# A selective-scan block: sums over the state issued in threes, one PSUM bank for states, nine of 24 products on GpSimd

## The chip, the cores and the metric

The kernel runs on one core of a Trainium2 chip. The metric is the device time of one execution in microseconds, the median of several runs. A profile is one further execution, taken by the hardware profiler.

## The reference, cut to what matters

The model has several blocks one after another on an input of 4 images, 96 channels, 64 x 64 pixels. The change lies in the first one, a selective scan over the 4096 pixels in four directions (K=4, rows, columns and both backwards), for 192 channels (DI) with 16 states each (N):

```python
def step(hst, inp):
    ut, dt_, bt, ct = inp
    dA = jnp.exp(dt_[..., None] * A[None])
    hst = hst * dA + (dt_ * ut)[..., None] * bt[:, :, None, :]
    y = jnp.einsum('bkdn,bkn->bkd', hst, ct)
    return (hst, y)
h0 = jnp.zeros((b, K, DI, N), jnp.float32)
_, ys = jax.lax.scan(step, h0, (u_t, d_t, B_t, C_t))
```

`delta` and u give the decay exp(delta A) and the input delta u B of each state; y is the sum over the 16 states of the state times C. The four directions are added, normalised over the channels and projected back to 96 channels. A block of three convolutions (1x1 to 576 channels, 3x3 by channel, 1x1 back) follows; then come a spectral block, an attention block and two feed-forward blocks, which the change doesn't touch.

## The kernel before, in words

For each of the four images, `scan_block` makes u by a convolution on TensorE (lines 230 to 254), then `scan_chunks` does the scan, `scan_output` the normalisation and projection, and `conv_block` the convolutions. After the four images the rest of the model runs image by image (line 698 on). 

`scan_chunks` works through 32 steps an image: 4 directions, each with 8 chunks of 512 pixels. A tile of 128 partitions holds 32 channels with 4 states each, so a step has 24 tiles: j runs over the four groups of states, i over the six groups of channels, t = 6 j + i. For each t (lines 347 to 367):

- ScalarE writes exp(delta A) into a PSUM bank `da` (line 353; two banks, names `ps_da`);
- GpSimd multiplies delta u with B into `db` (line 355; three buffers);
- VectorE scans h = h da + db along the 512 pixels (line 357). For the t in `POOL_C` (seven of 24) the state h goes to SBUF (`hs`, two buffers), for the others to a PSUM bank (`ps_h`, two banks);
- ScalarE copies the last column of h into `after`, the start of the next chunk (line 362; not in the last chunk of a direction);
- h is multiplied with C into `hc` (line 364; three buffers), on GpSimd for the t in `POOL_C`[...], on VectorE for the others;
- TensorE multiplies `hc` with a constant of 128 x 32 that adds the four states of each channel, and adds up over j in PSUM (line 367): the channels of i go to the quarter 32 (i mod 4) of the 128 columns, in bank `y01` for i under 4 and in `y2` for 4 and 5.

At a step's end VectorE adds `y01` and `y2` to the sums `ya` and `yb` over the directions (lines 373 and 374). Beside a step, `prepare` makes delta and delta u of the next one: matmuls into banks `mm` (lines 286, 287 and 297), ScalarE's copy and softplus (lines 289 and 300 to 302), two VectorE instructions for each half of the channels (lines 304 and 306), and writes to DRAM; from there they and B and C are loaded again, spread over the partitions (lines 315 and 323), from SP's queue.

Nobody writes out the order of the instructions. The program gives each engine's operations with their data, and a scheduler orders each engine's queue ahead of time: of the instructions that it holds for ready it takes the one that comes earliest in the program. It takes a free buffer for each tile, or makes the first writer wait for the release of an old one. In the run each engine follows its queue in this fixed order.

[...] Before, the function `bank` takes two for each name unless it is told otherwise: `mm`, `da` and `h` two each, `y01` and `y2` one each. `h` also serves `scan_output` (the variance, lines 390 and 391) and `conv_block` (the 3x3 convolution of two of the five tiles on TensorE, line 434), and `mm` the sums of the last convolution (line 448).

Of the kernel before, what the change touches and what calls it, by code (L numbers as in the profile page):

```python
# [17 lines left out]
F32 = mybir.dt.float32  # L18
# [13 lines left out]
CH = 512  # L32
# [2 lines left out]
NTOK = L // 128  # L35
NI, NJ = DI // 32, NS // 4
NE1 = NE + 1
POOL_C = (2, 5, 9, 12, 16, 19, 23)
ROWS1 = [128, 128, 128, 128, 64]
PE_CONV = (0, 1)  # L40

# [33 lines left out]
def hybrid_kernel(ctx: ExitStack, tc: tile.TileContext, a: dict):  # L75
# [40 lines left out]
    with tc.tile_pool(name="ca", bufs=1) as ca, tc.tile_pool(name="xa", bufs=1) as xa, tc.tile_pool(  # L116
        name="psa", bufs=2, space=PSUM
    ) as psa, tc.tile_pool(name="dr", bufs=3, space=bass.MemoryType.DRAM) as dr:
        def bank(tag, bufs=None):
            return psa.tile([128, CH], F32, name=f"ps_{tag}", tag=tag, bufs=bufs)  # L120

        cst = ca.tile([128, NCA], F32, name="cst_a")
        nc.sync.dma_start(cst, a["cst_a"])
# [154 lines left out]
        def scan_chunks(ua, ub, ya, yb, wk):  # L278

            steps = [(k, n, NCH - 1 - n if k >= 2 else n) for k in range(K) for n in range(NCH)]  # L280

            def prepare(at):

                k, _, c = steps[at]
                p = bank("mm")
                mm(p[:NE], lhsT=sel_a[:, k, :], rhs=view(ua, k, c), start=True, stop=False)
                mm(p[:NE], lhsT=sel_b[:, k, :], rhs=view(ub, k, c), start=False, stop=True)
                xd = xds[at % 2]
                nc.scalar.copy(xd[:NE], p[:NE])  # L289
                bc = dr.tile([2 * NS, CH], F32, name="dram_bc")  # L290
                nc.sync.dma_start(bc, xd[: 2 * NS])
                delta = dr.tile([DI, CH], F32, name="dram_delta")
                du = dr.tile([DI, CH], F32, name="dram_du")
                for u, lo, hi in ((ua, 0, 128), (ub, 128, DI)):
                    m = hi - lo
                    p = bank("mm")
                    mm(p[:m], lhsT=dtw[:, k, lo:hi], rhs=xd, start=True, stop=True)  # L297

                    z = wk.tile([m, CH], F32, name=f"z{lo}", bufs=1)
                    act(z, p[:m], AF.Abs)  # L300
                    act(z, z, AF.Exp, scale=-1.0)
                    act(z, z, AF.Ln, bias=1.0)
                    d = wk.tile([m, CH], F32, name=f"delta{lo}", bufs=1)
                    nc.vector.scalar_tensor_tensor(d, p[:m], 0.0, z, ALU.max, ALU.add)
                    g = wk.tile([m, CH], F32, name=f"du{lo}", bufs=1)
                    nc.vector.tensor_mul(split(g), split(d), view(u[:m], k, c))
                    nc.sync.dma_start(delta[lo:hi], d)
                    nc.sync.dma_start(du[lo:hi], g)
                return {"bc": bc, "delta": delta, "du": du, "B": {}, "C": {}, "d": {}, "g": {}}

            def load_states(s, j):

                for name, at in (("B", 4 * j), ("C", NS + 4 * j)):
                    t = wk.tile([128, CH], F32, name=f"rep_{name}", bufs=5)
                    nc.sync.dma_start(t, s["bc"][at : at + 4].unsqueeze(0).to_broadcast([32, 4, CH]))
                    s[name][j] = t

            def load_channels(s, i):

                for name, of in (("d", "delta"), ("g", "du")):  # L320
                    t = wk.tile([128, CH], F32, name=f"rep_{name}", bufs=9)
                    src = s[of][32 * i : 32 * i + 32].unsqueeze(1).to_broadcast([32, 4, CH])
                    nc.sync.dma_start(t, src)
                    s[name][i] = t

            def first_loads(s):
                load_states(s, 0)
                for i in range(NI // 2):
                    load_channels(s, i)

            cur = prepare(0)
            first_loads(cur)
            for j in range(1, NJ):
                load_states(cur, j)
            for i in range(NI // 2, NI):
                load_channels(cur, i)
            before = None
            for at, (k, n, c) in enumerate(steps):
                nxt = None
                if at + 1 < len(steps):  # L340
                    nxt = prepare(at + 1)
                    first_loads(nxt)
                order = slice(None, None, -1) if k >= 2 else slice(None)
                end = 0 if k >= 2 else CH - 1
                after = wk.tile([128, NI * NJ], F32, name="state") if n < NCH - 1 else None
                y01, y2 = bank("y01", 1), bank("y2", 1)
                for j in range(NJ):
                    for i in range(NI):
                        t = j * NI + i
                        pool_c = t in POOL_C  # L350
                        av = (k * NI + i) * NJ + j
                        da = bank("da")
                        act(da, cur["d"][i], AF.Exp, scale=aneg[:, av : av + 1])  # L353
                        db = wk.tile([128, CH], F32, name="db", bufs=3)
                        nc.gpsimd.tensor_mul(db, cur["g"][i], cur["B"][j])  # L355
                        h = wk.tile([128, CH], F32, name="hs") if pool_c else bank("h")
                        nc.vector.tensor_tensor_scan(  # L357
                            h[:, order], da[:, order], db[:, order],
                            0.0 if n == 0 else before[:, t : t + 1], ALU.mult, ALU.add,
                        )  # L360
                        if after is not None:
                            nc.scalar.copy(after[:, t : t + 1], h[:, end : end + 1])  # L362
                        hc = wk.tile([128, CH], F32, name="hc", bufs=3)
                        (nc.gpsimd if pool_c else nc.vector).tensor_mul(hc, h, cur["C"][j])  # L364
                        y = y01 if i < 4 else y2
                        q = 32 * (i % 4)
                        mm(y[q : q + 32], lhsT=cst[:, CA["stack"]], rhs=hc, start=j == 0, stop=j == NJ - 1)  # L367
                        if nxt is not None and j == NJ - 1 and i < NI // 2:
                            load_channels(nxt, NI // 2 + i)
                    if nxt is not None and j < NJ - 1:  # L370
                        load_states(nxt, j + 1)
                before = after
                nc.vector.tensor_add(view(ya, k, c), view(ya, k, c), split(y01))
                nc.vector.tensor_add(view(yb[:64], k, c), view(yb[:64], k, c), split(y2[0:64]))
                cur = nxt

        def scan_output(xt, ya, yb, wk):

            for c in range(NCH):
# [6 lines left out]
                qb = wk.tile([128, CH], F32, name="qb", tag="rep_g", bufs=9)  # L386
                act(qa, pa, AF.Square)
                act(qb[:64], pb[:64], AF.Square)
                v = bank("h")
                mm(v[:C], lhsT=mean_a, rhs=qa, start=True, stop=False)  # L390
                mm(v[:C], lhsT=mean_b[:64], rhs=qb[:64], start=False, stop=True)
                r = wk.tile([C, CH], F32, name="rb", tag="db", bufs=3)
# [7 lines left out]
        def conv_block(b, xt):  # L400

            with tc.tile_pool(name="h1", bufs=1) as hp, tc.tile_pool(name="wk1", bufs=3) as wk:
# [21 lines left out]
                for c in range(NCH):  # L424
                    h2 = []
                    for t, rows in enumerate(ROWS1):
# [2 lines left out]
                            return h1[t][:, c * RPC + dy : c * RPC + dy + RPC, dx : dx + W]  # L429

                        if t in PE_CONV:
                            src = bank("h")
                            for i in range(9):
                                mm(src, lhsT=diag[t][:, i, :], rhs=tap(i), start=i == 0, stop=i == 8)  # L434
                        else:
# [395 lines left out]
```

## Time and profile before

| | |
|---|---|
| median of 3 runs | 8842.88 us |
| lowest, highest | 8838.6, 8844.06 us |
| the profiled execution | 8844.98 us |
| its span, from the first instruction to the last | 8843.2 us |
| VectorE (DVE) busy | 6875.4 us, 78% |
| TensorE (PE) busy | 6434.1 us, 73% |
| GpSimd (POOL) busy | 5323.4 us, 60% |
| ScalarE (ACT) busy | 4124.7 us, 47% |
| steps of the scan, from the first to the last end of one in each image | 214.8 to 1578.9, 2042.3 to 3408.7, 3871.8 to 5234.5, 5697.9 to 7061.0 us |

In the lines of the profile, a group reads: line, engine, operation, what it writes and reads, shapes, how many; then its busy time in us and the mean of one in ns; then the idle time of that engine just ahead of these instructions, with what ended most of it. A timeline line reads: start and length in us, then the engine and the same names; "[0.23 <-ACT state L362]" is idle time ahead of it and what ended it. PEld is TensorE's loading of weights.

### The profile page before, as it was taken

What the parts mean: (1) busy time and instruction counts of PE and PEld (TensorE: products, weight loads), DVE (VectorE), ACT (ScalarE), POOL (GpSimd) and SP (SyncE); (2) the same over time, 40 slices, a digit from 0 to 9 for tenths busy, and PEclk for the clock granted to TensorE, in tenths of its full rate; (3) what the DMA queues carried; (4) which work ended last, traced back from release to release, by engine and by line L of the source; (5) the groups of instructions that cost most, each with busy time, mean ns of one, the idle gap of its engine ahead of it and who ended that gap; (6) DMA issues with size and microseconds to landing.
All of it is one profiled execution on the core that took longest, in us unless ns stands there. A gap on an engine that the chain in (4) does not pass through costs nothing. (4 is left out here: it accounts for less than half of the span.)

```text
span 8843.2 us, 79675 instructions
## 1 busy us (share of the span) xinstructions
PE 6434.1 (73%) x22508; PEld 1840.2 (21%) x22508; DVE 6875.4 (78%) x8002; ACT 4124.7 (47%) x8408; POOL 5323.4 (60%) x4290
## 2 busy tenths in 40 slices
PE   7666666986666668876666679866666698787887
PEld 1000000320000002310000013100000136264553
DVE  3999999729999997479999976499999973343333
ACT  2544544315444444144444442354454434757557
POOL 2999999108998993069989960399899801100001
PEclk9988988998898889989888889898898899898988
DMA  2444443004444440034444420244444301000000
GB/s 91 139 137 138 140 138 124 4 23 155 138 138 139 139 136 30 14 128 141 138 138 138 138 63 15 93 142 138 138 140 138 96 6 52 15 2 15 1 9 8
DMA packets 444922, 821.50 MB, mean 93 GB/s; under 512 B 53718, under 2 KB 55740, under 8 KB 443452
## 3 DMA queue, kind: packets, MB, share of 16 engines
q1 hardware_dynamic: 444476, 816.40, 30.0%
q8 instruction: 177, 2.90, 0.1%
q14 instruction: 269, 2.20, 0.1%
HBM read 694.55 MB, written 121.63 MB: 92 GB/s over the span
## 5 line engine op out<-in xcount | busy, mean ns | idle before, releaser
L367 PE MATMUL ps_y<-hc,cst_a 128*32 128x512 f32 x6144 | 3139.5, 713 | 1920.0 <-DVE hc L364 1226.3
L355 POOL TENSOR_TENSOR db<-rep_g,rep_B 128x512 f32<-128x512 f32 x3072 | 4045.3, 1351 | 287.3 <-DVE ps_h L357 233.2
L357 DVE TENSOR_TENSOR_SCAN ps_h<-ps_da,state,db 128x512 f32<-128x512 f32 x1904 | 2370.8, 1266 | 12.8 <-ACT state L362 11.8
L353 ACT ACTIVATE ps_da<-rep_d,aneg 128x512 f32<-128x512 f32 x3072 | 2127.6, 693 | 310.8 <-DVE ps_h L357 225.9
L364 DVE TENSOR_TENSOR hc<-ps_h,rep_C 128x512 f32<-128x512 f32 x2176 | 1406.9, 667 | 38.3 <-ACT state L362 31.6
L367 PEld LDWEIGHTS ps_y<-hc,cst_a 128*32 128x32 f32 x6144 | 439.3, 116 | 4655.6 <-DVE hc L364 2318.5
L364 POOL TENSOR_TENSOR hc<-hs,rep_C 128x512 f32<-128x512 f32 x896 | 1141.9, 1274 | 300.3 <-DVE hs L357 211.4
L362 ACT COPY state<-ps_h 128x1 f32<-128x1 f32 x1904 | 299.9, 158 | 1593.8 <-DVE ps_h L357 1593.1
L357 DVE TENSOR_TENSOR_SCAN hs<-ps_da,state,db 128x512 f32<-128x512 f32 x784 | 986.8, 1259 | 5.3 <-ACT ps_da L353 4.0
L688 POOL CAST hq<-acc 128x512 fp8e5<-128x512 f16 x192 | 122.9, 664 | 1372.7 <-DVE acc L687 1368.7
L440 DVE SCALAR_TENSOR_TENSOR acc<-h,cols,acc 128x512 f32<-128x512 f32 (+1 forms) x768 | 529.9, 740 | 5.9
L434 PE MATMUL ps_h<-h,diag 128*128 128x512 f32 x1152 | 504.4, 595 | 0.0
L362 ACT COPY state<-hs 128x1 f32<-128x1 f32 x784 | 149.7, 191 | 541.5 <-DVE hs L357 540.8
L234 POOL MEMSET ub<- 64x4096 f32 x4 | 14.0, 3506 | 593.2 <-PE ps_h L434 585.8
L260 DVE TENSOR_SCALAR ya<-ua,ds_a 128x4096 f32<-128x4096 f32 x4 | 22.1, 5530 | 434.2 <-PE ps_da L249 434.2
L357 DVE TENSOR_TENSOR_SCAN ps_h<-ps_da,db 128x512 f32<-128x512 f32 x272 | 322.1, 1207 | 14.7 <-ACT ps_da L353 12.1
L259 POOL MEMSET yb<- 64x4096 f32 x4 | 14.0, 3506 | 509.1 <-PE ps_da L249 509.1
L297 PE MATMUL ps_mm<-xd,dtw 128*128 128x512 f32 (+1 forms) x512 | 302.3, 675 | 14.7 <-ACT xd L289 14.1
L247 PE MATMUL ps_mm<-xp,taps 128*128 128x512 f32 x576 | 292.3, 630 | 17.9 <-DVE xp L214 14.2
L300 ACT ACTIVATE z<-ps_mm 128x512 f32<-128x512 f32 (+1 forms) x256 | 151.1, 590 | 282.5 <-PE ps_mm L297 281.6
L434 PEld LDWEIGHTS ps_h<-h,diag 128*128 128x128 f32 x1152 | 215.3, 189 | 286.4 <-issue 286.4
L555 PE MATMUL psb_mm<-sq,cst_b 128*96 128x512 f32 x256 | 184.6, 824 | 116.9 <-ACT sq L553 116.7
(214 smaller groups left out, 6858.9 us busy)
## 6 DMA issues: line engine op xcount, KB each, us to landing
rep_d<-dram_delta SPq DMA_DIRECT2D x768, 256.0 KB, 3.7
rep_g<-dram_du SPq DMA_DIRECT2D x768, 256.0 KB, 4.1
rep_B<-dram_bc SPq DMA_DIRECT2D x512, 256.0 KB, 3.0
rep_C<-dram_bc SPq DMA_DIRECT2D x512, 256.0 KB, 3.4
dram_delta<-delta SPq DMA_DIRECT2D x128, 256.0 KB, 3.4
dram_du<-du SPq DMA_DIRECT2D x128, 256.0 KB, 2.0
dram_delta<-delta SPq DMA_DIRECT2D x128, 128.0 KB, 2.3
dram_du<-du SPq DMA_DIRECT2D x128, 128.0 KB, 3.8
```

The source lines that it names most:

```text
L247: mm(pa[e], lhsT=taps[:, t, 0:128], rhs=rhs[e], start=t == 0, stop=t == 8)
L297: mm(p[:m], lhsT=dtw[:, k, lo:hi], rhs=xd, start=True, stop=True)
L300: act(z, p[:m], AF.Abs)
L353: act(da, cur["d"][i], AF.Exp, scale=aneg[:, av : av + 1])
L355: nc.gpsimd.tensor_mul(db, cur["g"][i], cur["B"][j])
L357: nc.vector.tensor_tensor_scan(h[:, order], da[:, order], db[:, order], 0.0 if n == 0 else before[:, t : t + 1], ALU.mult, ALU.add,)
L362: nc.scalar.copy(after[:, t : t + 1], h[:, end : end + 1])
L364: (nc.gpsimd if pool_c else nc.vector).tensor_mul(hc, h, cur["C"][j])
L367: mm(y[q : q + 32], lhsT=cst[:, CA["stack"]], rhs=hc, start=j == 0, stop=j == NJ - 1)
L434: mm(src, lhsT=diag[t][:, i, :], rhs=tap(i), start=i == 0, stop=i == 8)
L440: nc.vector.scalar_tensor_tensor(acc, tap(i), col("wd", 9 * t + i, slice(0, rows)), acc, ALU.mult, ALU.add)
L555: mm(v[:C], lhsT=mean, rhs=q, start=True, stop=True)
```

## The change

Four things change together. `POOL_C` has nine t instead of seven. `bank` gives three banks to `mm`, two to `da` and one to every other name, `h` among them, and no longer looks at the count that is passed. The buffers `hs` go from two to three, `hc` from three to seven. And the sums of line 367 are no longer given one by one behind their product: three are gathered and given together, the last first, and the other two are put behind it in TensorE's queue. The three i of such a group lie in three different column quarters. `scan_output` and `conv_block` take `mm` where they took `h`.

```diff
-POOL_C = (2, 5, 9, 12, 16, 19, 23)
+POOL_C = (1, 4, 7, 9, 12, 15, 17, 20, 23)
...
         def bank(tag, bufs=None):
-            return psa.tile([128, CH], F32, name=f"ps_{tag}", tag=tag, bufs=bufs)
+            return psa.tile([128, CH], F32, name=f"ps_{tag}", tag=tag, bufs={"mm": 3, "da": 2}.get(tag, 1))
...
                 y01, y2 = bank("y01", 1), bank("y2", 1)
+
+                def state_sums(hcs, j):
+                    with ExitStack() as behind:
+                        while hcs:
+                            i, hc = hcs.pop()
+                            q = 32 * (i % 4)
+                            y = y01 if i < 4 else y2
+                            m = mm(y[q : q + 32], lhsT=cst[:, CA["stack"]], rhs=hc, start=j == 0, stop=j == NJ - 1)
+                            behind.enter_context(tc.issue_after(m.ins))
+
+                hcs = []
                 for j in range(NJ):
                     for i in range(NI):
...
-                        h = wk.tile([128, CH], F32, name="hs") if pool_c else bank("h")
+                        h = wk.tile([128, CH], F32, name="hs", bufs=3) if pool_c else bank("h")
...
-                        hc = wk.tile([128, CH], F32, name="hc", bufs=3)
+                        hc = wk.tile([128, CH], F32, name="hc", bufs=7)
                         (nc.gpsimd if pool_c else nc.vector).tensor_mul(hc, h, cur["C"][j])
-                        y = y01 if i < 4 else y2
-                        q = 32 * (i % 4)
-                        mm(y[q : q + 32], lhsT=cst[:, CA["stack"]], rhs=hc, start=j == 0, stop=j == NJ - 1)
+                        hcs.append((i, hc))
+                        if len(hcs) == 3:
+                            state_sums(hcs, j)
...
-                v = bank("h")
+                v = bank("mm")
...
-                            src = bank("h")
+                            src = bank("mm")
```

## The prediction

> **What bounds the kernel now.** I read the page's list of costliest groups first, then the busy time of each engine over the stretches, then the timeline of one step, then one place at the start of the second image where VectorE runs tightly.
>
> The groups say what one of the 128 steps (4 images, 4 directions, 8 chunks) is made of: 24 exponents on ScalarE, 24 products with B on GpSimd, 24 scans and 17 products with C on VectorE, 7 products with C on GpSimd.
>
> ```profile
> L355 POOL TENSOR_TENSOR db<-rep_g,rep_B 128x512 f32<-128x512 f32 x3072 | 4045.3, 1351 | 287.3 <-DVE ps_h L357 233.2
> L357 DVE TENSOR_TENSOR_SCAN ps_h<-ps_da,state,db 128x512 f32<-128x512 f32 x1904 | 2370.8, 1266 | 12.8 <-ACT state L362 11.8
> L364 DVE TENSOR_TENSOR hc<-ps_h,rep_C 128x512 f32<-128x512 f32 x2176 | 1406.9, 667 | 38.3 <-ACT state L362 31.6
> L364 POOL TENSOR_TENSOR hc<-hs,rep_C 128x512 f32<-128x512 f32 x896 | 1141.9, 1274 | 300.3 <-DVE hs L357 211.4
> ```
>
> The reader is to see that GpSimd has idle time ahead of its instructions (287 and 300 us, mostly until VectorE is done) and VectorE almost none. The busy time over the scan stage of the first image, from its first step's end to its last's, and over what follows it up to the second image's, says the same (columns: stretch, length, then busy us of PE, PEld, DVE, ACT and POOL):
>
> ```profile
> 214.00:1579.00 1365.00, 894.98 (x1717) 129.30 (x1715) 1343.54 (x1451) 660.06 (x1586) 1237.34 (x959) 0.89 0.43 133
> 1579.00:2042.00 463.00, 418.97 (x946) 135.54 (x946) 223.78 (x314) 131.83 (x210) 56.33 (x61) 0.93 0.12 37
> ```
>
> VectorE is busy for 1343.5 of 1365 us, GpSimd for 1237.3. By the 31 intervals between the adds of line 374 a step takes 43.96 us on the mean of the four images: VectorE busy 43.29 and idle 0.67, GpSimd busy 39.87 and idle 4.09, ScalarE busy 21.3. The scan stages bound 128 x 43.96 = 5627 of the 8843 us, and in them **VectorE** is the bound.
>
> The timeline shows how VectorE stays full: two scans, then their two products, so that something else always stands between a scan and its own product.
>
> ```profile
> 704.47 0.67 DVE L364 TENSOR_TENSOR hc<-ps_h,rep_C 128x512 f32<-128x512 f32 x1
> 705.05 2.46 DVE L357 TENSOR_TENSOR_SCAN ps_h<-ps_da,state,db 128x512 f32<-128x512 f32 x2
> 707.41 1.27 DVE L364 TENSOR_TENSOR hc<-ps_h,rep_C 128x512 f32<-128x512 f32 x2
> 708.60 1.28 DVE L357 TENSOR_TENSOR_SCAN hs<-ps_da,state,db 128x512 f32<-128x512 f32 x1
> ```
>
> An instruction starts before the one ahead of it ends: product to product 0.59 us from start to start at 0.67 each, scan to scan 1.19 at 1.27. So a follower starts 0.07 to 0.08 us ahead of the end. Two PSUM banks for `ps_h` make this order possible.
>
> Where nothing stands between, it looks different:
>
> ```profile
> 2003.65 1.23 DVE L357 TENSOR_TENSOR_SCAN ps_h<-ps_da,db 128x512 f32<-128x512 f32 x1 [4.04 <-ACT ps_da L353]
> ...
> 2004.91 0.16 ACT L362 COPY state<-ps_h 128x1 f32<-128x1 f32 x1 [0.75 <-DVE ps_h L357]
> ...
> 2005.10 0.69 DVE L364 TENSOR_TENSOR hc<-ps_h,rep_C 128x512 f32<-128x512 f32 x1 [0.23 <-ACT state L362]
> ```
>
> The product waits for ScalarE's copy of the last state out of the same bank, and starts 0.225 us after the scan's end instead of 0.08 before it: **0.305 us** lost. This is the number on which my forecast rests. A second one: a VectorE instruction that waits for the one just ahead of it on VectorE starts 0.036 us after its end (line 398 behind line 397, 32 times), or 0.104 us after when it has a second wait as well (line 695 behind 694, 60 times).
>
> ```profile
> 1593.55 0.68 DVE L397 TENSOR_TENSOR rb<-rb,ps_y 96x512 f32<-96x512 f32 x1 [6.05 <-PE ps_y L396]
> 1594.27 0.75 DVE L398 SCALAR_TENSOR_TENSOR xt<-rb,wout_bias,xt 96x512 f32<-96x512 f32 x1
> ```
>
> Against the usual overlap of 0.075 that is 0.11 or 0.18 us lost.
>
> **What the Trainium skill says.** "PSUM — Partial Sum Buffer", PSUM bank collisions raise a hardware error: two engines must not touch one bank and partition quadrant at once, reads included. So the copy and the product, both of one bank, stand in a row; the 0.225 us above agrees. "VectorE: DVE Perf Modes", The DRAIN you can't avoid: a read right after a write on the same engine still needs a semaphore, and the semaphore "costs nothing extra here". The trace agrees on the need and not on the price (0.11 to 0.18 us). "SBUF — State Buffer", Who interferes with whom: VectorE with two SBUF inputs contends with GpSimd's reads, with one it doesn't. The trace agrees: line 306 (both inputs in SBUF) takes 1.15 us, and 233 of the GpSimd instructions over 1.4 us lie beside it; the others take 1.27. "TensorEngine Tiling (Array Packing)", Key Properties: tiles run independently. In the trace four matmuls of two sums at 718.96 take 1.05 us, as two of one sum do.
>
> **The change, part by part** (per step, then times 128).
>
> *Two more products to GpSimd.* VectorE loses 2 x 0.59 = 1.18 us: 43.29 to 42.11. GpSimd gains 2 x 1.27 = 2.54: 39.87 to 42.41. Alone, this brings the two engines level, and it could win up to 1.18 x 128 = 151 us.
>
> *One bank for `h`.* Fifteen scans a step still write PSUM, now all into one bank. So each goes: scan, ScalarE's copy, product, next scan into that bank. The next such scan must wait for the product (I see the scans of before wait for VectorE's own semaphore too, but for an older product, so it costs nothing). That makes 30 places a step where VectorE can stand: 15 ahead of a product, 0.305 us each, and 15 ahead of the next scan. For the latter the trace has no case with a bank reused at once; the bounds are 0 (in-order engine, wait already met), 0.11 and 0.18. I take 0.18, because a scan has waits for GpSimd and ScalarE besides, as line 695 has a second one. All open: 15 x 0.305 + 15 x 0.18 = 4.58 + 2.70 = 7.28 us.
>
> What can stand in these places is what needs no `h` bank: nine scans into SBUF, and six others (two each of lines 304 and 306, and lines 373 and 374). Fifteen instructions for thirty places. The list (1, 4, 7, 9, 12, 15, 17, 20, 23) leaves groups of PSUM, PSUM, SBUF six times and PSUM, SBUF three times. In the longer group the SBUF scan comes behind the second PSUM scan; it can't come earlier, as `da` has two banks and the exponent for it starts only when the first scan of the group is over (0.26 us with the copy, then 0.70). I let the nine scans cover nine products (2.75 us), and the six others half products and half scans (6 x 0.24 = 1.46). Left: 7.28 - 2.75 - 1.46 = 3.07 us. Bounds: with the six all ahead of products and 0.11 a scan, 15 x 0.11 = 1.65; with the six covering nothing, 4.53.
>
> *Sums in threes.* The same 6144 matmuls of 0.71 us on TensorE, which is busy for about two thirds of the stage; three sums now lie beside each other. What hides it: nothing on VectorE reads them but lines 373 and 374. Seven `hc` buffers hold a waiting group of three and four more (some 7 us of work), so no product waits; before, such waits were 27 us on GpSimd and 4.5 on VectorE in all. The last group ends with GpSimd's product of t=23, and line 373 must now await it too: line 374 waits 36 us in all today, so 0 to 36 us; I take 0, because the next step's scans can be put ahead of it. PE's queue: while a group waits for its last product, the matmuls of `prepare` stand behind it, at most about two products (4 us); `prepare` has most of a step. No DMA is moved.
>
> *Banks of `mm`.* Three instead of two; the convolution's and output's tiles move from `h` to it. TensorE bounds that stage and has at most 8 us of waits on ScalarE there to gain; a third bank less in line 434's stage may cost as much. Taken as 0, bounds -8 and +20. The passed count for `y01` and `y2` is now ignored, but the default gives them one bank as before.
>
> *Sum.* Per step -1.18 + 3.07 = +1.89, period 45.85; GpSimd at 42.41 stays under it. 128 x 1.89 = 242. In the last chunk of each direction (16 steps) there is no copy, and some three open products cost 0.11 instead of 0.305: -9. Total +233 on the profiled 8845 us (span 8843.2): 9078. The median of the runs is 2 us lower: **9076**.
>
> **The rivals.** *GpSimd takes over* (0.10). Its 42.41 us of work come in order, and each product with C there waits for its scan: 300 us in all before, 2.35 a step. If that stays, a step takes 44.8, +0.8, 8945 in all. Against it: those waits exist because GpSimd runs ahead of VectorE, which it would no longer do. *Faster* (0.12): the scan behind its product isn't held at all, because VectorE works in order, and the scheduler puts its fifteen fillers ahead of the fifteen products. Then a step takes 42.11 + 0.67 = 42.8 and all of it 8692; it decides once the open waits of a step sum to under 1.18 us, so at 0.18 each at six or fewer. For it speaks that the order is found by a scheduler that fills gaps; against it, that own-engine waits cost 36 to 104 ns past the end everywhere I find them. *The fillers don't fill* (0.10): 4.53 left, +3.35 a step, 9272, and 9308 with line 373 waiting. *It cancels* (0.04): within 0.2%, about what a measurement of this kernel can tell from no change.
>
> **How the numbers follow.** My case has 0.64, with 8960 to 9200 of its own. Slower by over 0.2%: 0.64 + 0.10 + 0.10 = 0.84; within: 0.04; faster: 0.12. The range 8890 to 9280 begins at the lower bound of the waits (1.65 - 1.18 = +0.47 a step, 8903) with a little for `mm`, and reaches to 4.53 left; it leaves out the faster case, the equal one and part of the fourth, under 0.2.
>
> **What would show it.** In the profile after: line 357 into `ps_h` x1680 and into `hs` x1008; idle time ahead of VectorE's line 364 until ScalarE's line 362 in hundreds of us instead of 38; gaps of 0.1 us between a product and the next scan; VectorE busy about 42 of 46 us, GpSimd busy 42.4 a step without bounding. Wrong if VectorE stays over 98% busy (then the waits are covered), or if its idle time ends on `db` of line 355 (then GpSimd bounds).

## The result, and the profile after

| | before | after |
|---|---|---|
| median | 8843.47 us | 9519.76 us |
| lowest, highest | 8838.6, 8846.52 us | 9512.12, 9527.04 us |
| ratio, 95% interval | | 1.0765 [1.0747, 1.0784] |
| the profiled execution, its span | 8844.98, 8843.2 us | 9520.95, 9519.0 us |
| period of a step | 43.96 us | 49.04 us |

The change costs 676 us; the forecast was +233. Lines 353, 355, 357, 362, 364 and 367 of before are now 366, 368, 370, 375, 377 and 356, and the adds 373 and 374 are 386 and 387.

The groups on the page of after, those shown of before:

```profile
L368 POOL TENSOR_TENSOR db<-rep_g,rep_B 128x512 f32<-128x512 f32 x3072 | 4041.2, 1334 | 927.7 <-DVE hs L370 464.2
...
L370 DVE TENSOR_TENSOR_SCAN ps_h<-ps_da,state,db 128x512 f32<-128x512 f32 x1680 | 2141.2, 1274 | 62.0 <-DVE hc L377 1.9
L377 DVE TENSOR_TENSOR hc<-ps_h,rep_C 128x512 f32<-128x512 f32 x1920 | 1320.8, 688 | 342.4 <-ACT state L375 323.1
L377 POOL TENSOR_TENSOR hc<-hs,rep_C 128x512 f32<-128x512 f32 x1152 | 1484.4, 1289 | 21.4 <-DVE hs L370 21.4
```

GpSimd now waits 928 us ahead of line 368 instead of 287, and 949 us instead of 587 with its products with C, so it bounds nothing. Most of it is for VectorE's scans (what waited, for what; us in total, times, longest):

```profile
POOL db L368 <- DVE hs L370: 464.2, 705, 1.6
POOL db L368 <- DVE ps_h L370: 389.1, 180, 3.6
```

VectorE's products wait 342 us, of which 323 end with ScalarE's copy of the last state; before, these were 38 and 32. The stretches of the first image (columns as in the prediction):

```profile
218.00:1739.00 1521.00, 608.16 (x1696) 73.09 (x1696) 1375.21 (x1380) 660.62 (x1571) 1308.31 (x1019) 0.56 0.37 118
1739.00:2218.00 479.00, 417.77 (x964) 136.31 (x964) 235.16 (x322) 139.46 (x225) 61.70 (x65) 0.92 0.12 40
```

The scan stage is 156 us longer, with VectorE busy for 1375 of 1521 us instead of 1344 of 1365. TensorE's granted clock there fell from 0.89 to 0.56. The same list for VectorE names a second loser:

```profile
DVE hc L377 <- ACT state L375: 323.1, 1294, 2.4
...
DVE ya L386 <- PE ps_y L356: 166.0, 121, 1.6
```

Line 373 of before waited 0.2 us in all. The timeline of after shows the order on VectorE:

```profile
713.19 0.69 DVE L377 TENSOR_TENSOR hc<-ps_h,rep_C 128x512 f32<-128x512 f32 x1 [0.23 <-ACT state L375]
713.86 1.28 DVE L370 TENSOR_TENSOR_SCAN hs<-ps_da,state,db 128x512 f32<-128x512 f32 x1
...
715.06 1.27 DVE L370 TENSOR_TENSOR_SCAN ps_h<-ps_da,state,db 128x512 f32<-128x512 f32 x1
...
716.36 0.16 ACT L375 COPY state<-ps_h 128x1 f32<-128x1 f32 x1 [0.40 <-DVE ps_h L370]
...
716.55 0.69 DVE L377 TENSOR_TENSOR hc<-ps_h,rep_C 128x512 f32<-128x512 f32 x1 [0.23 <-ACT state L375]
717.35 1.29 DVE L370 TENSOR_TENSOR_SCAN ps_h<-ps_da,state,db 128x512 f32<-128x512 f32 x1
```

The scan into SBUF stands between a product and the next PSUM scan, so it covers the cheap wait (0.18 us). The dear one, a PSUM scan followed by its own product, stays open: 716.33 to 716.55, the prediction's 0.23 us gap.

**A budget of the step.** For each pair of neighbours on VectorE I took the start of the second less the end of the first, plus the usual overlap of 0.076 us, and summed by kind of pair between the first and the last add of line 387 of each image. Before, VectorE loses 0.70 us a step in this way; after, 6.40:

| after, per step | places | each | sum |
|---|---|---|---|
| PSUM scan, then its product | 11.81 | 0.283 | 3.34 |
| last PSUM scan put ahead, then line 386 | 0.97 | 1.41 | 1.36 |
| product, then PSUM scan | 5.06 | 0.186 | 0.94 |
| product, then SBUF scan | 8.97 | 0.055 | 0.50 |
| line 304, then a product | 1.35 | 0.193 | 0.26 |

The 0.283 is a mean of two kinds of place. Where ScalarE copies the last state it is 0.30 us (median 0.301); in the last chunk of a direction, which has no copy, it is 0.11 to 0.18, 0.161 on the mean. For the next PSUM scan the medians are 0.18 with copies and 0.21 without.

The period grew by 5.08 us; over the 124 intervals that is 630 us. The other 46 lie outside: each of the three stretches between images is 12 to 16 us longer, some 41 in all, and start and tail are 5 longer.

### The profile page after: what moved, and what is told of

It reads as the page before. It is cut to its first block, busy times and chain, and to the rows that moved or that the text cites. A ratio compares the mean times of both kernels' runs of the same rounds, so it can differ in the third digit from the quotient of the medians.

```text
span 9519.0 us, 78407 instructions
## 1 busy us (share of the span) xinstructions
PE 5265.6 (55%) x22508; PEld 1613.1 (17%) x22508; DVE 7046.1 (74%) x7746; ACT 4156.6 (44%) x8408; POOL 5627.6 (59%) x4546
## 5 line engine op out<-in xcount | busy, mean ns | idle before, releaser
L356 PE MATMUL ps_y<-hc,cst_a 128*32 128x512 f32 x6144 | 1898.2, 1016 | 3412.2 <-DVE hc L377 2184.8
L370 DVE TENSOR_TENSOR_SCAN ps_h<-ps_da,state,db 128x512 f32<-128x512 f32 x1680 | 2141.2, 1274 | 62.0 <-DVE hc L377 1.9
L377 DVE TENSOR_TENSOR hc<-ps_h,rep_C 128x512 f32<-128x512 f32 x1920 | 1320.8, 688 | 342.4 <-ACT state L375 323.1
L377 POOL TENSOR_TENSOR hc<-hs,rep_C 128x512 f32<-128x512 f32 x1152 | 1484.4, 1289 | 21.4 <-DVE hs L370 21.4
L370 DVE TENSOR_TENSOR_SCAN hs<-ps_da,state,db 128x512 f32<-128x512 f32 x1008 | 1290.0, 1280 | 10.5 <-issue 2.3
L356 PEld LDWEIGHTS ps_y<-hc,cst_a 128*32 128x32 f32 x6144 | 200.4, 137 | 5119.6 <-DVE hc L377 2466.0
L375 ACT COPY state<-hs 128x1 f32<-128x1 f32 x1008 | 191.9, 190 | 1221.6 <-DVE hs L370 1220.8
L447 PE MATMUL ps_mm<-h,diag 128*128 128x512 f32 x1152 | 504.5, 595 | 0.0
L286 PE MATMUL ps_mm<-ua,sel_a 128*38 128x512 f32 x256 | 206.2, 895 | 184.6 <-DVE delta L304 184.4
L447 PEld LDWEIGHTS ps_mm<-h,diag 128*128 128x128 f32 x1152 | 215.1, 189 | 286.7 <-issue 286.7
```

The lines of the kernel that those rows point to most:

```text
L356: m = mm(y[q : q + 32], lhsT=cst[:, CA["stack"]], rhs=hc, start=j == 0, stop=j == NJ - 1)
L370: nc.vector.tensor_tensor_scan(h[:, order], da[:, order], db[:, order], 0.0 if n == 0 else before[:, t : t + 1], ALU.mult, ALU.add,)
```

## The experiments

Theory: the one `h` bank makes VectorE stand, at the prices predicted, but the queue's order leaves the dear places open, and the threes put a second wait ahead of line 386. Rivals: the nine products (GpSimd) or the crowding of preparations in the first steps carry the loss. Lines in the fences are numbered as in the kernel that ran. In the text the two adds of a step's end are lines 386 and 387 for kernels made from after, 373 and 374 for those made from before. Every median has a run of before beside it, between 8838 and 8845 us.

**Parts undone.** *Two banks for `h` again*, all else as after:

```diff
-bufs={"mm": 3, "da": 2}.get(tag, 1)
+bufs={"mm": 2, "da": 2, "h": 2}.get(tag, 1)
-                v = bank("mm")
+                v = bank("h")
-                            src = bank("mm")
+                            src = bank("h")
```

> The kernel after with its bank part undone: two banks each for mm, da and h, and the variance and the 3x3 convolution in h again; threes and nine of 24 stay. Theory (the single bank): its waits, 4.8 us of a step's 5.7 us of added waits on VectorE, go away, and with them the later stages' 46 us: 4.8 x 128 + 46 = 660 us less, about 8860 to 8930. Rival (the sums in threes hold VectorE at lines 386 and 387 and through TensorE's low clock): at most the order of instructions changes, above 9300. Rival (GpSimd with nine products bounds as soon as VectorE doesn't): about 42.4 + 2.4 = 44.8 us a step, 8950, with VectorE's idle time ending on db.

Measured: 9298.56 us, 1.0518 [1.0503, 1.0534], period 47.44. Far above before, so the bank isn't all. The waits on VectorE are down to 1.63 us a step; instead, line 306 has grown. Its durations (least, median, most, in ns) in this kernel:

```profile
L306 DVE TENSOR_TENSOR du<-delta,ub x128: 672/4772/5382, 146.8 to 7414.6; 64x512 f32<-64x512 f32 x128
```

And in the kernel before:

```profile
L306 DVE TENSOR_TENSOR du<-delta,ub x128: 671/1198/2130, 158.7 to 6975.2; 64x512 f32<-64x512 f32 x128
```

The timeline of the two-bank kernel shows one case:

```profile
712.53 3.79 POOL L368 TENSOR_TENSOR db<-rep_g,rep_B 128x512 f32<-128x512 f32 x3
713.08 5.35 DVE L306 TENSOR_TENSOR du<-delta,ub 64x512 f32<-64x512 f32 x1
...
716.19 1.35 POOL L377 TENSOR_TENSOR hc<-hs,rep_C 128x512 f32<-128x512 f32 x1
...
720.31 2.55 POOL L368 TENSOR_TENSOR db<-rep_g,rep_B 128x512 f32<-128x512 f32 x2 [2.77 <-DVE ps_h L370]
```

An instruction that can take 0.67 us takes 5.35, over four GpSimd instructions that follow without a gap; it ends 0.89 us after the last of them (717.54 to 718.43), as if it had begun only then. GpSimd waits for VectorE in its turn (2.77 us). This points to the reads that VectorE's two SBUF inputs share with GpSimd, and is tested below.

*The sums one by one again* (`hc` keeps seven buffers):

```diff
-                        hcs.append((i, hc))
-                        if len(hcs) == 3:
-                            state_sums(hcs, j)
+                        y = y01 if i < 4 else y2
+                        q = 32 * (i % 4)
+                        mm(y[q : q + 32], lhsT=cst[:, CA["stack"]], rhs=hc, start=j == 0, stop=j == NJ - 1)
```

> The kernel after with the sums given one by one again (seven hc buffers stay). Theory (single bank): only VectorE's wait ahead of line 386's add goes, 1.36 us a step against 0.3 before: 1.06 x 128 = 136 us less, about 9385; TensorE's granted clock in the scan goes back up from 0.55 toward 0.9. Rival (the threes are the main cost): 8850 to 9000.

9389.27 us, 1.062 [1.0604, 1.0636]: 131 less than after. The wait moved to line 387 and fell to 0.73 us a step.

*Seven products again*, `POOL_C = (2, 5, 9, 12, 16, 19, 23)`, one bank and threes kept:

> The kernel after, with seven of 24 products on GpSimd as before, all else as after (one bank for h, sums in threes). My theory, that inside a kernel with one bank the nine products save time since two PSUM scans fewer have to wait: 9850 to 9950 us. The rival, that the nine cost here as they do with two banks (347 us there): 9200 to 9350 us.

9812.78 us, 1.1103 [1.1086, 1.1119]. So inside the one-bank kernel the nine products save 293 us. That is close to two products at 0.59 us and two pairs of places at 0.283 + 0.186: 2.12 us a step, 271.

**Parts alone, on before.** *The nine products* (with `hs` in three buffers):

```diff
-POOL_C = (2, 5, 9, 12, 16, 19, 23)
+POOL_C = (1, 4, 7, 9, 12, 15, 17, 20, 23)
```

> The kernel before with nine of 24 products on GpSimd (and three hs buffers), nothing else. With the bank part undone, line 306 (both inputs in SBUF) took 3.05 us instead of 1.06, up to 5.35 beside four GpSimd instructions in a row. Theory (GpSimd without gaps keeps the shared read path from VectorE's two-input instruction): the same here, 2 x 2.0 us a step more and 1.18 less, about +2.8 x 128 = +360, 9150 to 9250, line 306 at 2.5 to 3.1 us. Rival (the long line 306 comes of the order in which the threes leave GpSimd, not of the ninth product): line 306 near 1.1 us and 8700, the gain that the prediction gave to this part alone.

9188.59 us, 1.0381 [1.0352, 1.0409], as expected. The change that was to save 151 us costs 347 where two banks are kept.

*The bank part* (the new `bank`, and `mm` where `h` was used elsewhere):

> The kernel before with the bank part alone (one bank for h, three for mm, variance and 3x3 convolution in mm). Theory (waits at the one bank, priced by the kernel after): 17 products at 0.283 less some four that others cover, 10 next scans at 0.186, 7 at 0.055: 3.7 + 1.9 + 0.4 = 6.0 us a step, 128 x 6.0 + 46 = 810 more, about 9650, slower than the whole change, because two more PSUM scans a step pay the waits. Rival (the bank costs only what undoing it gave back, 221 us): 9060.

9802.6 us, 1.1086 [1.107, 1.1103]: more than expected. It loses 3.70 us a step ahead of products and 1.72 ahead of PSUM scans, as there are 17 such scans and fewer fillers. What goes beyond the expectation lies ahead of line 374 (0.97 us) and of products behind lines 304 and 306 (1.10).

*The threes* (`state_sums` and `hc` in seven buffers):

> The kernel before with the sums in threes alone (seven hc buffers). Theory: VectorE's add of y01 then waits for the last group, at TensorE's low clock; undoing the threes in the kernel after gave 131 us back, so about +1.0 us a step, 8950 to 9000. Rival (the threes cost only where VectorE is held by the one bank anyway): 8840 to 8870.

8958.13 us, 1.013 [1.0114, 1.0147], in the expected range.

Alone the parts cost 347, 961 and 119 us, 1427 in sum; together 676. Most of the difference is the nine products: they cost 347 with two banks and save 293 with one.

**The order.** VectorE's order is set by hand to PSUM scan, SBUF scan of the next t, product of the first, and the products otherwise as in after:

```diff
+                        with ExitStack() as behind:
+                            if pool_c and todo:
+                                behind.enter_context(tc.issue_after(scan.ins))
+                            scan = nc.vector.tensor_tensor_scan(
...
-                        hc = wk.tile([128, CH], F32, name="hc", bufs=7)
-                        (nc.gpsimd if pool_c else nc.vector).tensor_mul(hc, h, cur["C"][j])
+                        todo.append((i, j, pool_c, h))
+                        if t + 1 not in POOL_C:
+                            for i_, j_, p_, h_ in todo:
+                                hc = wk.tile([128, CH], F32, name="hc", bufs=7)
+                                with ExitStack() as behind:
+                                    if pool_c and not p_:
+                                        behind.enter_context(tc.issue_after(scan.ins))
+                                    (nc.gpsimd if p_ else nc.vector).tensor_mul(hc, h_, cur["C"][j_])
```

> The kernel after with VectorE's order pinned to the one that the prediction assumed: PSUM scan, then the SBUF scan of the next t, then the product of the PSUM scan. In the kernel after, the SBUF scan stands ahead of the PSUM scan, where it covers 0.186 less 0.055 us of waiting, and the 0.283 us ahead of the product stay open. Theory (waits at a single bank, covered or not by the order): nine times 0.15 to 0.18 us a step, 175 to 207 us less, about 9320 to 9345. Rival (the time is GpSimd's or ScalarE's lateness, and the waits only show it): no change, 9520.

9233.26 us, 1.0443 [1.0428, 1.0459]: 286 less than after, more than expected. Its timeline:

```profile
700.60 1.29 DVE L373 TENSOR_TENSOR_SCAN ps_h<-ps_da,state,db 128x512 f32<-128x512 f32 x1
701.80 1.26 DVE L373 TENSOR_TENSOR_SCAN hs<-ps_da,state,db 128x512 f32<-128x512 f32 x1
...
702.98 0.67 DVE L386 TENSOR_TENSOR hc<-ps_h,rep_C 128x512 f32<-128x512 f32 x1
...
703.78 1.29 DVE L373 TENSOR_TENSOR_SCAN ps_h<-ps_da,state,db 128x512 f32<-128x512 f32 x1
```

The product at 702.98 follows without a gap; the price is now paid between it and the next scan (703.65 to 703.78). By the budget: 5.06 open products at 0.279, 12.68 open scans at 0.202, and 0.35 instead of 1.36 us ahead of the add. So the places themselves give back 0.75 us a step (4.78 to 4.03), some 95 us, about half of what was expected; the two adds give back 0.98 us, some 125. The rest is shorter waits behind line 304 and VectorE's own work. The add waits less, as GpSimd's product for the step's last SBUF scan now starts 0.16 us after that scan instead of 2.56 (medians): no two products with B stand ahead of it. The expectation had the direction and not the split.

*The same order with the sums one by one*, that is, the prediction's two assumptions made true:

> The kernel after with VectorE's order pinned as in a_order (PSUM scan, SBUF scan of the next t, then the product of the first) and the sums given one by one. These are the two things that the prediction took for granted. My theory, that the two costs lie in different places except for the wait ahead of line 386, part of which the pinned order took already: 9110 to 9180 us, best guess 9150. If the two simply add (286 and 131 less): 9102. The rival, that pinning the order has removed what the threes cost, so that nothing more is left to gain: 9233.

9215.2 us, 1.0414 [1.0398, 1.043]: only 18 less. The rival was right here: once the order is pinned, the threes cost nearly nothing.

**The step's end.** *Four more matmuls for each group* (into a quarter of `y2` that nobody reads), so that TensorE isn't idle between groups:

```diff
+                        if len(hcs) < 3:
+                            for _ in range(2):
+                                mm(y2[96:128], lhsT=cst[:, CA["stack"]], rhs=hc, start=True, stop=True)
```

> The kernel after with four more matmuls a group of three, into a quarter of y2 that nobody reads, on the group's first two hc: TensorE has work between the groups. Theory (the low clock lengthens the last group ahead of line 386 from 1.05 to 1.93 us): the granted clock in the scan rises from 0.55 to 0.9, the wait ahead of the add falls by up to 0.88 us a step, 110 us less, about 9410. Rival (the add waits for GpSimd's last product, not for TensorE): clock up, time 9520 or more.

9528.16 us, 1.0776 [1.076, 1.0792]: no gain, against the expectation. In the timeline of after, a step ends so:

```profile
701.42 1.28 DVE L370 TENSOR_TENSOR_SCAN hs<-ps_da,state,db 128x512 f32<-128x512 f32 x1
...
702.78 2.51 POOL L368 TENSOR_TENSOR db<-rep_g,rep_B 128x512 f32<-128x512 f32 x2 [0.68 <-DVE hs L370]
...
705.24 1.28 POOL L377 TENSOR_TENSOR hc<-hs,rep_C 128x512 f32<-128x512 f32 x1
...
706.57 1.93 PE L356 MATMUL ps_y<-hc,cst_a 128*32 128x512 f32 x6 [3.75 <-POOL hc L377]
...
708.58 1.25 DVE L386 TENSOR_TENSOR ya<-ya,ps_y 128x512 f32<-128x512 f32 x1 [1.34 <-PE ps_y L356]
```

The last SBUF scan of the step ends at 702.70; GpSimd makes two products with B, then the one with C, then TensorE the group, and the add comes at 708.58. With the extra matmuls a group looks so:

```profile
704.77 1.06 PE L356 MATMUL ps_y<-hc,cst_a 128*32 128x512 f32 x6
```

So that part of the mechanism holds: over the whole run the mean clock went from 0.69 to 0.96, a group from 1.93 to 1.06 us, the wait ahead of the add from 1.41 to 0.78. Steps of the middle of an image went from 47.5 to 46.7 us. But the first six steps of an image, with the preparations in them, grew from 353 to 374 us in sum, and took it back. The traces say how: in the first image, from 218 to 520 us, TensorE is now busy for 285 us instead of 200, ScalarE waits 73 us for the preparations' matmuls instead of 33, its copies of the last state come later, and VectorE's products wait 31 us for them instead of 12.

*t = 22 instead of 23 on GpSimd*, so that a step's last product is VectorE's:

> The kernel after with t = 22 instead of 23 on GpSimd, so that the last product of a step is VectorE's. My theory, that about half of the 1.36 us a step ahead of line 386 is GpSimd's last product and the rest TensorE's slow group: 9400 to 9460 us. The rivals: all of it is GpSimd's, 9346; none, 9520.

9359.46 us, 1.0572 [1.0547, 1.0597]: 160 less, about all of the wait; the expectation of half was wrong. GpSimd's product and TensorE's group stand one behind the other, so a shorter link of either kind shortens the wait: the faster group took off 0.6 us a step, this edit all. Its line in the groups has no wait left:

```profile
L386 DVE TENSOR_TENSOR ya<-ya,ps_y 128x512 f32<-128x512 f32 x128 | 122.4, 956 | 0.0
```

**Two more rivals.** *Without the copies*: each chunk starts from zeros, the state isn't carried.

```diff
-                after = wk.tile([128, NI * NJ], F32, name="state") if n < NCH - 1 else None
+                after = zst if n < NCH - 1 else None
...
-                        if after is not None:
-                            nc.scalar.copy(after[:, t : t + 1], h[:, end : end + 1])
```

> The kernel after without ScalarE's copies of the last state: every scan but those of a direction's first chunk starts from zeros, so the state isn't carried from chunk to chunk; everything else stays, the scan still reads its start from SBUF. Theory: the product then waits for its own engine alone, 0.11 us instead of 0.283, at 11.8 places in 7 of 8 chunks: about 230 us less, 9290. Rival (the wait is the same engine's own read after write, the copy is beside the point): no change within 40 us.

9334.74 us, 1.056 [1.0542, 1.0577]: 185 less. The place ahead of a product falls to 0.162 us, not to 0. That is what the last chunks of after show too (0.161), so VectorE's wait for its own scan remains, and of the 0.30 us of a place with a copy about 0.14 is the copy. The products gain 1.51 us a step; scans behind a product lose 0.81 of it again, and shorter waits elsewhere and less work give some back, hence less than the 230 expected.

*Preparations spread*: `prepare`'s VectorE instructions are held behind the last scan of the step before. In after, all of an image's preparations lie in its first six steps (seven to ten of line 306 in each instead of two), and these take 55 to 62 us.

```diff
+                    with ExitStack() as behind:
+                        if scan is not None:
+                            behind.enter_context(tc.issue_after(scan.ins))
+                        nxt = prepare(at + 1)
-                    nxt = prepare(at + 1)
```

> The kernel after, with the preparation's VectorE instructions held behind the last scan of the step before, so that two of its multiplications by u lie in each step instead of eight to ten in the first five. My theory, that the one bank for h makes the waits and that the preparations only fill them wherever they stand: 9460 to 9560 us, best guess 9480. The rival, that the crowding of the preparations into the first six steps is itself a cost (those steps are 55 to 62 us against 45.4 to 47.5 for the others): 9300 or less.

9554.58 us, 1.081 [1.0794, 1.0826]. Steps of 48 to 51 us all along, and the sum is no better: the crowding catches the eye in the timeline, but spreading the preparations gains nothing.

**The held line 306.** If it is the reads from SBUF, delta in PSUM must end it. In the two-bank kernel line 304 writes back into its PSUM bank, and line 306 reads from there:

```diff
-                    nc.vector.scalar_tensor_tensor(d, p[:m], 0.0, z, ALU.max, ALU.add)
+                    nc.vector.scalar_tensor_tensor(p[:m], p[:m], 0.0, z, ALU.max, ALU.add)
+                    nc.scalar.copy(d, p[:m])
...
-                    nc.vector.tensor_mul(split(g), split(d), view(u[:m], k, c))
+                    nc.vector.tensor_mul(split(g), split(p[:m]), view(u[:m], k, c))
```

> The kernel after with two banks each for mm, da and h (the run with 9299 us), and with delta kept in its PSUM bank: line 304 writes it back into the bank, ScalarE copies it to SBUF for the store, and line 306 reads it from PSUM, so that it has one SBUF input. Theory (line 306 is held by GpSimd at the shared read path): line 306 falls from 3.05 to 0.67 us, 2 x 2.4 x 128 = 610 us less, 8690. Rival (line 306 is long because of the strided view or of its place in the queue): line 306 stays over 2 us, 9300.

8812.84 us, 0.9966 [0.9953, 0.9979]: 486 less than with delta in SBUF, and below before, though 120 short of the expectation. Line 306 takes 0.77 us instead of 3.05 (net of the overlap), with its strided view unchanged, so the rival is out. The same edit *on before*:

> The kernel before with delta kept in its PSUM bank as above, nothing else. Theory: line 306 falls from 1.06 (with the overlap taken off) to 0.59 us, twice a step, 0.95 x 128 = 120 us less, 8720; GpSimd gets back the 0.6 us a step that it waits beside line 306. Rival (the ScalarE copy in the same bank holds VectorE): no gain or a loss, 8840 to 8900.

8824.93 us, 0.9981 [0.9974, 0.9989]: a seventh of the gain expected. Line 306 fell from 1.06 to 0.78 us only, 0.54 us a step, and longer waits ahead of the second add (0.72 us a step instead of 0.32) took most of that. On *the nine products alone*:

> The kernel before with nine products on GpSimd and delta kept in PSUM; two h banks, single sums. Theory (the ninth product's harm is line 306 at the shared read path, and the bank's and the threes' waits are the rest): VectorE 42.73 - 1.18 = 41.55, GpSimd 41.3, both nearly full, some 1.5 us of idle time: 43.0, about 8720 to 8760, against 9189 with line 306 reading SBUF. Rival (nine products are too many whatever line 306 reads): 8850 or more.

8910.38 us, 1.0078 [1.0063, 1.0093]: 278 less than with the nine products and delta in SBUF, so that most of what the nine cost goes with line 306's second SBUF input. Still slower than before, against the expectation: VectorE waits 126 us ahead of the second add (36 before), 108 ahead of products for ScalarE's copy (32) and 82 ahead of PSUM scans for GpSimd (3). *Eight products*, `POOL_C = (1, 4, 7, 10, 13, 16, 19, 22)`:

> The kernel before with eight products on GpSimd, t = 1, 4, 7, 10, 13, 16, 19, 22, and delta kept in PSUM. VectorE 42.73 - 0.59 = 42.1, GpSimd 40.0, idle about 1.0: 43.1, 8730, if the theory holds; the rival as for nine: 8830.

8959.56 us, 1.0132 [1.0117, 1.0147]: a clear miss. Between two PSUM scans in a row it loses 1.86 us a step. That is one long wait, of up to 3.7 us, in 88 steps, mostly for ScalarE's copy of the last state. In the one at 817 us ScalarE had stood for 2.9 us at the preparation's copy (line 289), which waits for TensorE, with the other copies and exponents queued behind. Whether all 88 arise so, and why not with nine products, stays open.

*The two-bank kernel with delta in PSUM and t = 22 for 23:*

> The two-bank version with nine products, sums in threes and delta kept in a PSUM bank, with t = 22 instead of 23 on GpSimd, so that the last product of a step is VectorE's. My theory, that the wait ahead of the two adds at a step's end is GpSimd's last product (0.7 us a step): 8750 to 8770 us. The rival, that the wait is TensorE's: 8812 us as with t = 23.

8727.12 us, 0.9875 [0.9858, 0.9891], the fastest of all and 113 us under the runs of before beside it, better than expected, but not by the way expected: the wait ahead of the two adds stayed (0.76 us a step, 0.69 with t = 23), and what fell were the waits ahead of SBUF scans (0.81 to 0.34) and of products (0.42 to 0.20). Line 306 (307 here), and the add:

```profile
L387 DVE TENSOR_TENSOR ya<-ya,ps_y 128x512 f32<-128x512 f32 x128 | 124.5, 972 | 82.2 <-PE ps_y L357 82.1
L307 DVE TENSOR_TENSOR du<-ps_mm,ua 128x512 f32<-128x512 f32 x128 | 106.8, 834 | 0.2
L307 DVE TENSOR_TENSOR du<-ps_mm,ub 64x512 f32<-64x512 f32 x128 | 106.6, 833 | 0.0
```

The 256 of line 307 take 0.66 to 1.02 us, with GpSimd busy for 40.8 of a step's 43.0 us. *And with the sums one by one:*

> The version with two h banks, nine products (22 for 23) and delta in PSUM, with the sums one by one instead of in threes. If the sums in threes still cost something there (0.70 us a step ahead of the adds at a step's end): 8650 to 8690 us. If it is the seven hc buffers that count and not the threes: the same as with threes, 8727. If TensorE's queue holds products up again: above 8750.

8943.05 us, 1.0115 [1.0098, 1.0132]. Here the threes save 216 us; TensorE's busy time a step goes from 29.3 to 20.2 us with them. In this kernel GpSimd's products wait 421 us, with the threes 147:

```profile
L365 POOL TENSOR_TENSOR hc<-hs,rep_C 128x512 f32<-128x512 f32 x1152 | 1473.6, 1279 | 420.9 <-DVE hs L358 256.4 <-PE ps_y L368 82.9 <-issue 53.4
```

The 83 us are waits for a free `hc` that TensorE still reads. That TensorE is the whole cause isn't shown, as the queue's order differs too.

## Why the prediction was right in kind and wrong in size

**Right.** The bound stays VectorE, with GpSimd at 42.1 us a step (42.41 predicted), and the product's wait for ScalarE's copy is the largest loss. The two prices held: 0.30 us against 0.305 ahead of a product with a copy (0.283 with the places without one), and 0.186 to 0.202 against 0.18 ahead of the next scan; 0 and 0.11 are excluded for the latter. The reason given for 0.18, a second wait, wasn't tested. Inside the one-bank kernel the nine products save 293 us, where the prices give 271.

**The step that failed** is "I let the nine scans cover nine products (2.75 us)". It took for granted that the queue would put an SBUF scan between a PSUM scan and that scan's own product. In the queue of after VectorE's scans and products stand in the program's order but for those around the adds: behind each PSUM scan comes its own product, at most with a preparation's instruction between. So all nine SBUF scans stand behind a product and cover nine of the cheap places. The data didn't ask for it. Scans, exponents and products with B go in the order of t, so they can be counted off against each other, and the SBUF scan at 713.86 had both inputs by 708.04, when the PSUM scan ahead of it hadn't begun:

```profile
706.46 2.58 POOL L368 TENSOR_TENSOR db<-rep_g,rep_B 128x512 f32<-128x512 f32 x2
...
707.34 0.70 ACT L366 ACTIVATE ps_da<-rep_d,aneg 128x512 f32<-128x512 f32 x1
...
711.67 1.29 DVE L370 TENSOR_TENSOR_SCAN ps_h<-ps_da,state,db 128x512 f32<-128x512 f32 x1
```

Of the 1152 SBUF scans 1134 had their inputs when the PSUM scan ahead of them ended. The prediction's ground, that the exponent starts when the first scan of the group is over, held (707.34, behind a scan that ended at 707.25); the queue didn't use the time. Pinning the order confirms it: no SBUF scan stands behind a product any more, and these places give back some 95 of the 286 us. Why the scheduler, ahead of time, held the product for the better choice isn't shown.

| us per step | predicted | after | order pinned, sums one by one (profiled at 9191 us) |
|---|---|---|---|
| VectorE's own work | 42.11 | 42.65 | 42.24 |
| ahead of products | 3 x 0.305 = 0.92 | 3.34 | 1.42 |
| ahead of PSUM scans | 12 x 0.18 = 2.16 | 0.94 | 2.35 |
| SBUF scans behind a product | 0 | 0.50 | 0 |
| ahead of the adds 386, 387 | 0 | 1.43 | 0.51 |
| the rest (before: 0.67) | 0.67 | 0.18 | 0.21 |
| period | 45.85 | 49.04 | 46.73 |

With the assumption made true the open places cost 3.77 us against 3.07 predicted, and the period is 0.88 us off instead of 3.19. Of the 443 us that the forecast fell short, some 210 lie at these places, 180 ahead of the adds and 46 outside the scans; VectorE's longer work and the smaller rest about cancel.

**The second failed step** is "I take 0" for line 373, with 36 us as the bound. It measured 166 (174 with line 387). Instructions of the next step were put ahead of the add, as foreseen (three scans and a product, from 702.62 on), but the chain behind the last SBUF scan was longer: two products with B queued ahead on GpSimd (2.51 us), its product with C (1.28), then the group (1.93), 5.9 us with the steps between. The 1.93 was read as 1.05 from four matmuls of two sums that lay among other work. The Trainium skill, "TensorE: Matmul & The Clock Gate", Part 1: The HAM clock gate, says that TensorE's clock is halved after an idle window of about 3.4 us. The trace of after fits: in the middle of the first image TensorE is idle for 3.2 to 5.5 us ahead of each group, the clock from 540 to 1700 us is 0.50, and a group takes 1.93 us; with the gaps filled it takes 1.06. That it needs a gap of 3.4 us isn't shown: in before's scan stages the clock fell to half for short times too, mostly with no gap over 3 us in the 7 us ahead. The bound should have been that chain, with what may be queued ahead on each engine, less the work that can be put ahead of the add.

**Smaller terms.** VectorE's own work is 0.5 us longer than predicted; products take 0.612 instead of 0.590 us net of the overlap, and line 306 1.17 instead of 1.06. Outside the scans 46 us went where the bound for `mm` was 20; with two `h` banks some 20 of them came back, and the rest isn't explained.

**The rivals.** "The fillers don't fill" (9272, or 9308 with line 373) was nearest, but by luck: its 4.53 us of open places are near the 4.78 measured, yet it too let the nine SBUF scans cover nine products and left the six other fillers useless, where it was the SBUF scans that covered little. "GpSimd takes over" was wrong for this kernel. With two banks the nine products did cost time, but not in the way it named: VectorE stayed the busier engine (45.9 of 47.5 us a step), with its own instruction held beside GpSimd's. The prediction cited the page on shared reads, and priced line 306 at 1.15 us as if a busier GpSimd left it alone; in after that nearly held (1.25 us).

## What to carry to other kernels

Where one bank takes the place of two, write out for each filler which of the two waits it will stand in, and don't count on the dearer one: here every SBUF scan stood in the cheaper, ready or not, until the order was pinned. For what ends a step, add up the whole chain behind the last scan, with what is queued ahead on each engine. A part's cost depends on the slack of the others: nine products cost 347 us beside two banks and saved 293 beside one, so test each part both alone and taken away. Before filling GpSimd to the brim, look for VectorE instructions with two SBUF inputs and move one input to PSUM.

## What the runs showed of the hardware

- A VectorE instruction with two SBUF inputs can be held for several GpSimd instructions in a row: line 306 took 4.77 us on the median of one half of the channels and 5.38 at most, instead of 0.67. "SBUF — State Buffer", Who interferes with whom, says that such an instruction contends with GpSimd's reads; that it loses several times running is what the two-bank run adds. With one input in PSUM it took 0.66 to 1.02 us beside a GpSimd that was busy for a larger share of the step (40.8 of 43.0 us, against 41.6 of 47.5).
- A product that follows its own scan without anything between loses 0.11 to 0.18 us (0.161 on the mean) by VectorE's own wait, and 0.30 if ScalarE copies a column out of the same bank in between. A scan into the bank that the product just ahead of it read loses 0.18 to 0.21 us.
- TensorE with its work in groups of three sums every 5.9 us ran at half its clock in the middle of the scan stage, and a group took 1.93 us instead of 1.06.
